# Four gelus that wait together for the last of four products

## The chip, the cores and the metric

The kernel runs on one core of a Trainium2 chip. A core has five engines with a queue of their own each: TensorE (PE; its weight loads are listed as PEld), VectorE (DVE), ScalarE (ACT), GpSimd (POOL) and SyncE (SP), which here only issues transfers. They meet through semaphores: an instruction can wait until a count is reached, and can raise a count when it is done. The metric is the time of one execution on the device in microseconds, lower is better.

## The reference, cut to what matters

The program is two layers of a graph network with attention and a mixture of experts, on 3125 nodes with 256 features. The change is in the last block of the second layer, a mixture of 8 experts of which each node uses two:

```
xn = layer_norm(x) * gamma + beta
logits = xn @ Wr + br                          # 8 logits a node
w = softmax of the two largest logits, 0 for the other experts
for e in range(8):
    h   = gelu(xn @ W1[e] + b1[e])             # 256 -> 512
    y_e = h @ W2[e] + b2[e]                    # 512 -> 256
    y  += y_e * w[..., e]
```

The kernel computes every expert for every node and weighs the results. All numbers are 32-bit floats.

## The kernel before, in words

Nodes lie in 25 tiles of 128 (the last has 53). The kernel makes two passes over the edges, one for each layer. A pass gathers, for each tile and each place in the nodes' edge lists, one row for every node from a table in memory (`gather`, L193, on GpSimd), and VectorE adds what came (L1356 folds the gathered rows, L1361 adds them to the tile's sum). The second pass runs from about 1590 us to the end. When a group of tiles has its sums, the rest of its work is put into a list of background jobs, and the pass does some of them after each handful of gathers, by a credit that the jobs' written costs use up.

There are 11 groups in the second pass. In order of work they have 4, 2, 4, 3, 3, 2, 2, 2, 1, 1 and 1 tiles. The jobs of a group (class `Group`) are: `sums_a` to `sums_c`, products of the graph part and a gelu (L2300 to L2309); `states_a` to `states_d`, the two normalizations, with square roots on ScalarE (L2327); `routes_a`, the transposes (L2370, L2371) and the eight logits (L2378); `routes_b`, the choice of two experts, with an exponential on ScalarE (L214); `shares`, a transpose of the weights (L2397, L2399) and the biases (L2425); then steps 0 to 9. The last four steps of a group are put between the first jobs of the next group.

Step i does three things in this order. `take` adds to x what the banks of earlier second products hold (L2450 for the biases, L2458 for an expert, VectorE). `hidden(i)` makes the first products of expert i for the whole group: 512 hidden features are four blocks of 128 (`FC` = 4), for each block two matmuls (one for each half of the 256 input features, L2408) fill one bank of PSUM, and ScalarE reads it through the gelu into `hT` (L2412). `outputs(i - 1)` makes the second products of the expert before (L2439): for each tile four matmuls, two tiles to a bank. A 32-bit matmul stands as two records in the trace, so `hidden` is 16 records and `outputs` 8 records for each tile.

The banks matter for the order. The pool `ps_mm` has four banks in turn; first products and the products of `sums_a` and `sums_b` share them. The second products use two other banks in turn (`bank`), and `hT` has three buffers. The order on VectorE and GpSimd is as the program is written (`manual_schedule`); the orders on TensorE and ScalarE are chosen by a planner from its own modelled times, with earlier written work first, so that an instruction which is ready sooner can be put ahead. ScalarE holds one table of functions at a time; gelu, exponential and square root need different ones, and a change of table is an instruction of its own (ACT_TABLE_LOAD).

Of the kernel before, what the change touches and what calls it, by code (L numbers as in the profile page):

```python
# [11 lines left out]
F32 = mybir.dt.float32  # L12
BF16 = mybir.dt.bfloat16
I32 = mybir.dt.int32
AF = mybir.ActivationFunctionType
# [5 lines left out]
P = 128  # L21
# [13 lines left out]
FC = F // P  # L35
# [65 lines left out]
def gps_kernel(ctx: ExitStack, tc: tile.TileContext, a, out):  # L101
    nc = tc.nc
    V, S, G, PE = nc.vector, nc.scalar, nc.gpsimd, nc.tensor
# [5 lines left out]
    ps_mm = ctx.enter_context(tc.tile_pool(name="ps_mm", bufs=4, space=PSUM))  # L109
# [1205 lines left out]

    def fast():
        fx = ExitStack()
        ek = fx.enter_context(tc.tile_pool(name="ek", bufs=1))  # L1320
# [175 lines left out]
        def hidden(ts):  # L1496
            n, at0 = len(ts) * P, ts[0] * P
            for i in range(2):
                hT = hTs[i] = f0h.tile([P, FC, 3 * P], F32, name=f"hT0_{i}", bufs=1)
                for f in range(FC):  # L1500
                    ph = ps_mm.tile([P, 512], F32, name="mm")
                    for c in range(2):
                        PE.matmul(  # L1503
                            ph[:, :n], w1[:, i, c, f * P : (f + 1) * P], xT[:, c, at0 : at0 + n],
                            start=(c == 0), stop=(c == 1),
                        )
                    S.activation(hT[:, f, :n], ph[:, :n], AF.Gelu, bias=b1[:, i, f : f + 1])

        def hidden_products(ts, i, ph=None):

            at0 = ts[0] * P
            ph = ps_mm.tile([P, 512], F32, name="mm") if ph is None else ph
            for f in range(FC):
                for c in range(2):
                    PE.matmul(
                        ph[:, f * P : (f + 1) * P], w1[:, i, c, f * P : (f + 1) * P], xT[:, c, at0 : at0 + P],
                        start=(c == 0), stop=(c == 1),
                    )
            return ph
# [45 lines left out]
        with ExitStack() as l0x:  # L1565
# [334 lines left out]
            def after0(g, tiles, accs):  # L1900
                last = g == len(GROUPS) - 1
                if last:
                    fin[0].accs = accs
                    return
                bg.extend(Fin0(tiles, accs).jobs())
                if g == SURE:
                    bg.extend(staged(guess(), (4.0, 3.0, 3.0, 2.0, 2.0, 2.0)))
                    for r in range(NX):
                        bg.extend(staged(relation(r), (1.5, 1.5)))
                for ts in GROUPS[: g + 1] if g == SURE else [tiles] if g > SURE else []:  # L1910
                    bg.append((5.0 * len(ts), lambda ts=ts: hidden(ts)))
                    if waiting:
                        bg.append(waiting.pop())
                    bg.append((4.0 * len(ts), lambda ts=ts: (outputs_a(ts), outputs_out(ts))))
                    waiting.append((1.0 * len(ts), lambda ts=ts: outputs_b(ts)))
                if g == len(GROUPS) - 2:
                    bg.append((4.0, lambda: None))
                    bg.append(waiting.pop())
                if g == len(GROUPS) - 2:
                    fin.append(Fin0(GROUPS[-1], None))  # L1920
                    bg.append((2.5, lambda: fin[0].products(0)))
# [21 lines left out]
            with tc.manual_schedule(engines={ET.DVE, ET.Pool, ET.PE, ET.Activation}):  # L1943
# [5 lines left out]
                phs = [hidden_products(ts, i) for i in range(2)]  # L1949
# [4 lines left out]
        with tc.If(again > 0):  # L1954
            w_full, rank = settled
            pick = f0k.tile([P, 2, NX], F32, name="pick")
            for i in range(2):
                V.tensor_scalar(pick[:, i, :], rank[:, 0, :], float(i), None, op0=ALU.is_equal)
            load_pair(pick)
            tmp = f0k.tile([P, NX], F32, name="tmp_c")  # L1960
            V.tensor_tensor(tmp, w_full[:, 0, :], pick[:, 0, :], op=ALU.mult)
            V.reduce_sum(w_first, tmp, axis=AX.X)
            for ts in GROUPS:
                k = len(ts)
                mv = small.tile([P, 4, 2], F32, name="mv1")
                rs = small.tile([P, 4], F32, name="rs1")
                for j, t in enumerate(ts):
                    V.tensor_tensor(x[:, t, :], x[:, t, :], bet, op=ALU.subtract)
                    stats(x[:, t, :], mv[:, j, :])
                rstd(mv[:, :k, :], rs[:, :k])  # L1970
                for j, t in enumerate(ts):
                    normalize(xt_tok[:, t, :], x[:, t, :], mv[:, j, :], rs[:, j : j + 1])
                    V.tensor_tensor(x[:, t, :], x[:, t, :], bet, op=ALU.add)
                    to_xT(t, xt_tok[:, t, :])
                if ts == GROUPS[-1]:
                    for i in range(2):
                        hidden_products(ts, i, phs[i])
                else:
                    hidden(ts)
                    outputs_a(ts)  # L1980
                    outputs_out(ts)
                    outputs_b(ts)
# [176 lines left out]
        with ExitStack() as l1x:  # L2159
# [18 lines left out]
            b1 = l1w.tile([P, NX, FC], F32, name="b1")  # L2178
# [107 lines left out]
            class Group:  # L2286
# [115 lines left out]
                def hidden(self, e):  # L2402
                    n, at0 = self.n, self.at0
                    hT = self.hT[e] = f1.tile([P, FC, 4 * P], F32, name="hT1")
                    for f in range(FC):
                        ph = ps_mm.tile([P, 512], F32, name="mm")
                        for c in range(2):
                            PE.matmul(  # L2408
                                ph[:, :n], w1s[e][:, c, f * P : (f + 1) * P], xT[:, c, at0 : at0 + n],
                                start=(c == 0), stop=(c == 1),  # L2410
                            )
                        S.activation(hT[:, f, :n], ph[:, :n], AF.Gelu, bias=b1[:, e, f : f + 1])  # L2412

                def bank(self):
                    turn[0] += 1
# [164 lines left out]
    with tc.If(unfit < 1):  # L2580
        fast()
# [78 lines left out]
```

## Time and profile before

| | |
|---|---|
| median of 4 runs | 2956.26 us (2943.61 to 2969.74) |
| profiled execution | 2937.95 us, span 2936.2 us |
| granted TensorE clock, mean of the span | 0.768 |
| gelus of the experts, L2412 | 352, 167.6 us busy, 496 ns each |
| table loads put down to L2412 | 27, 1283 ns each |
| first products, L2408 | 1408 records, 432.7 us busy |
| second products, L2439 | 1600 records, 405.4 us busy |
| weighted sums, L2458 | 200, 88.1 us busy, 478 ns each |

A row of the timeline gives start, duration, engine, line and operation, then the output and inputs by the program's names, the shapes, the number of instructions merged into the row, and in brackets how long the engine stood idle before it and what ended that. The ends of matmuls are modelled; their starts are recorded. A row of the waits gives the engine and line that waited, what it waited for, the total in microseconds, how often and the longest. "Issue" means that the profile shows nothing that was waited for, and "remote" that a semaphore ended the wait and no recorded instruction explains when.

### The profile page before, as it was taken

The page shows a single profiled execution, that of the slowest core. Times are in us where ns is not written, and L with a number is a line of the kernel's source. Part 1 is how long each engine was busy: PE and PEld are TensorE (multiplying, and loading weights), DVE is VectorE, ACT ScalarE, POOL GpSimd, SP SyncE. Part 2 cuts the span into 40 slices and gives each one's busy share as a digit, 9 for nine tenths or more (in the row PEclk, how much of TensorE's full clock was granted, in tenths as well). Part 3 has the DMA queues.
Part 4 walks back from the last instruction along what each step waited for, and adds up shares of the span by engine and source line. Part 5 has one row for each costly group of instructions (what it writes and reads, how often), then busy time and mean ns, then how long its engine had stood idle before and what let it go on. Part 6 is the DMA issues. An engine that isn't in the chain of part 4 may idle for free.

```text
span 2936.2 us, 20996 instructions
## 1 busy us (share of the span) xinstructions
PE 1880.8 (64%) x6033; PEld 1177.0 (40%) x6033; DVE 1256.6 (43%) x3537; ACT 558.3 (19%) x1275; POOL 1725.0 (59%) x1830
## 2 busy tenths in 40 slices
PE   4355667403473745275997259867887686767877
PEld 3222333202341423144443125544554464555666
DVE  7443545436333424344664333335343334344342
ACT  5122221001110101021321112112112121222233
POOL 5566665676757565753046745555666566665551
PEclk9666767655786766686998668878887888887878
DMA  6533333343323233332356532222332232232220
GB/s 189 126 92 90 93 90 102 94 107 108 95 77 102 69 99 81 100 81 57 144 201 233 162 104 76 84 79 84 89 93 85 72 86 83 83 90 75 79 81 16
DMA packets 125962, 290.09 MB, mean 99 GB/s; under 512 B 41386, under 2 KB 63982, under 8 KB 122632
## 3 DMA queue, kind: packets, MB, share of 16 engines
q0 software_dynamic: 83184, 230.02, 28.7%
q1 hardware_dynamic: 38122, 55.88, 5.8%
q10 hardware_dynamic: 4526, 2.71, 0.3%
q8 instruction: 51, 0.84, 0.1%
q14 instruction: 79, 0.65, 0.1%
HBM read 249.07 MB, written 39.41 MB: 98 GB/s over the span
## 4 chain that ended last, share of the span: by engine, by line
PE 22%; issue 9%; another core or an unknown queue 8%; POOL 5%; DVE 5%; ACT 2%; DMA 1%; SPq 0%; DVEq 0%; POOLq 0%; ACTq 0%
PE mm L2408 9%; PE py L2439 6%; POOL gt L193 5%; PE mm L188 3%; DVE gt L1356 1%; DMA gt<-htab_f,idx2g 1%; PE pctx L2247 1%; DVE bnst L162 1%; PE pt L2378 1%; DVE x L2458 1%; DVE acc L1361 0%; PE mm L2302 0%; PE py L2425 0%; DVE x L2343 0%
## 5 line engine op out<-in xcount | busy, mean ns | idle before, releaser
L193 POOL DMA_INDIRECT gt<-btab,idx x814 | 802.5, 986 | 444.7 <-issue 222.9
L193 POOL DMA_INDIRECT gt<-htab_f,idx2g x742 | 732.1, 987 | 477.0 <-DVE acc L1361 249.0
L2408 PE MATMUL mm<-xT,w 128*128 128x256 f32 (+4 forms) x1408 | 432.7, 458 | 108.0 <-issue 59.5
L2439 PE MATMUL py<-w,hT 128*128 128x256 f32 (+1 forms) x1600 | 405.4, 406 | 78.6 <-issue 41.7
L1356 DVE TENSOR_TENSOR gt<-gt 128x256 f32<-128x256 f32 (+1 forms) x767 | 410.1, 535 | 70.2 <-DMA gt<-htab_f,idx2g 23.3
L2439 PEld LDWEIGHTS py<-w,hT 128*128 128x128 f32 (+1 forms) x1600 | 317.6, 202 | 159.1 <-issue 79.7
L2408 PEld LDWEIGHTS mm<-xT,w 128*128 128x128 f32 x1408 | 267.4, 217 | 249.5 <-issue 159.2
L2458 DVE SCALAR_TENSOR_TENSOR x<-py,wf,x 128x256 f32<-128x256 f32 x200 | 88.1, 478 | 495.8 <-remote 284.1
L2412 ACT ACTIVATE hT<-mm,b 128x256 f32<-128x256 f32 (+4 forms) x352 | 167.6, 496 | 588.0 <-PE mm L2408 262.9
L188 PE MATMUL mm<-w_rel,xT 128*128 128x512 f32 x400 | 178.1, 603 | 8.0 <-ACT xT L183 7.4
L1361 DVE TENSOR_TENSOR acc<-acc,gt 128x256 f32<-128x256 f32 x371 | 158.3, 427 | 23.3 <-DVE gt L1356 6.6
L1532 PE MATMUL mm<-w,hT 128*128 128x256 f32 x400 | 126.4, 474 | 61.7 <-issue 53.6
L1503 PE MATMUL mm<-xT,w 128*128 128x384 f32 (+2 forms) x320 | 110.8, 513 | 80.6 <-issue 34.9
L1532 PEld LDWEIGHTS mm<-w,hT 128*128 128x128 f32 x400 | 90.7, 237 | 111.4 <-issue 85.2
L188 PE MATMUL mm<-w_qkv,xT 128*128 128x512 f32 (+1 forms) x200 | 101.0, 627 | 38.9 <-issue 25.5
L188 PE MATMUL pt<-w_own,xT 128*128 128x256 f32 x100 | 42.2, 547 | 125.7 <-DVE acc L1845 71.1
L1503 PEld LDWEIGHTS mm<-xT,w 128*128 128x128 f32 x320 | 69.7, 242 | 121.1 <-issue 56.5
L188 PEld LDWEIGHTS mm<-w_rel,xT 128*128 128x128 f32 x400 | 75.9, 193 | 102.4 <-issue 88.2
L1863 PE MATMUL pmean<-ones,xt 128*128 128x1 f32 (+1 forms) x100 | 21.5, 319 | 131.3 <-DVE xt L171 130.8
L193 POOL DMA_INDIRECT gt<-htab_f,soon x72 | 73.6, 1023 | 46.3 <-issue 20.2
L1620 DVE COPY slots<-gt 128x4 f32<-128x4 f32 (+1 forms) x214 | 36.8, 172 | 119.4 <-DMA gt<-btab,idx 112.7
L188 PEld LDWEIGHTS pt<-w_own,xT 128*128 128x128 f32 x100 | 24.6, 271 | 140.6 <-DVE acc L1845 73.1
(436 smaller groups left out, 2117.2 us busy)
## 6 DMA issues: line engine op xcount, KB each, us to landing
htab_f<-hs SPq DMA_DIRECT2D x25, 1024.0 KB
gt<-btab,idx POOLq DMA_INDIRECT x814
gt<-htab_f,idx2g POOLq DMA_INDIRECT x742
w<-in_f_W_dram SPq DMA_DIRECT2D x20, 512.0 KB
ntab<-x SPq DMA_DIRECT2D x5, 640.0 KB
btab<-bs SPq DMA_DIRECT2D x5, 640.0 KB
x<-in_x_dram SPq DMA_DIRECT2D x4, 640.0 KB
otab<-xn SPq DMA_DIRECT2D x16, 128.0 KB
```

The source lines that it names most:

```text
L162: V.bn_stats(out=st, in_=src)
L188: PE.matmul(ps, lhs[:, c, t * P : (t + 1) * P], w[:, c, :], start=start and c == 0, stop=stop and c == 1)
L193: G.indirect_dma_start(out=dst, out_offset=None, in_=table, in_offset=bass.IndirectOffsetOnAxis(ap=idx, axis=0))
L1356: V.tensor_tensor(gt[:, :h, :], gt[:, :h, :], gt[:, m - h : m, :], op=op)
L1361: V.tensor_tensor(acc, own(t) if i == 0 else acc, gt[:, 0, :], op=op)
L1503: PE.matmul(ph[:, :n], w1[:, i, c, f * P : (f + 1) * P], xT[:, c, at0 : at0 + n], start=(c == 0), stop=(c == 1),)
L1532: PE.matmul(py[:, i * D : (i + 1) * D], hTs[i][:, f, j * P : (j + 1) * P], w2[:, i, f, :], start=False, stop=(f == FC - 1), skip_group_che ...
L1620: V.tensor_copy(slots_of[t][:, U - 1 - k1 : U - 1 - k0], gw[:, : k1 - k0, D])
L2408: PE.matmul(ph[:, :n], w1s[e][:, c, f * P : (f + 1) * P], xT[:, c, at0 : at0 + n], start=(c == 0), stop=(c == 1),)
L2412: S.activation(hT[:, f, :n], ph[:, :n], AF.Gelu, bias=b1[:, e, f : f + 1])
L2439: PE.matmul(py[:r, j * D : (j + 1) * D], hT[:, f, at : at + r], w2s[e][:, f, :], start=(f == 0), stop=(f == FC - 1),)
L2458: V.scalar_tensor_tensor(d, y, wf[:r, t, e : e + 1], d, op0=ALU.mult, op1=ALU.add)
```

## The change

The four banks of an expert are taken first and all eight matmuls are written ahead of the four gelus. Each gelu gets, beside its own bank, a wait for the last matmul of the last block. Since ScalarE then waits for the same count before the first gelu, the other three need no wait of their own, and of the four products only the last has to signal. The number of matmuls, of gelus and their sizes is as before.

```
+    def behind(ins, pe):
+        tc.add_manual_dep(
+            ins.ins, pe.ins.name, mybir.DependencyInfo(mybir.DependencyClass.Sync, mybir.DependencyReason.DATA),
+            reason="one signal for a row of products",
+        )
...
                 def hidden(self, e):
                     n, at0 = self.n, self.at0
                     hT = self.hT[e] = f1.tile([P, FC, 4 * P], F32, name="hT1")
-                    for f in range(FC):
-                        ph = ps_mm.tile([P, 512], F32, name="mm")
+                    phs = [ps_mm.tile([P, 512], F32, name="mm") for f in range(FC)]
+                    for f, ph in enumerate(phs):
                         for c in range(2):
-                            PE.matmul(
+                            end = PE.matmul(
                                 ph[:, :n], w1s[e][:, c, f * P : (f + 1) * P], xT[:, c, at0 : at0 + n],
                                 start=(c == 0), stop=(c == 1),
                             )
-                        S.activation(hT[:, f, :n], ph[:, :n], AF.Gelu, bias=b1[:, e, f : f + 1])
+                    for f, ph in enumerate(phs):
+                        got = S.activation(hT[:, f, :n], ph[:, :n], AF.Gelu, bias=b1[:, e, f : f + 1])
+                        behind(got, end)
```

## The prediction

> **What bounds the kernel now.** I read the table of busy time, the busy time by stretch, the waits of the second pass (from 1750 us to the end), and then the timeline of two engines around single experts. The four columns before the clock are busy time and instructions of TensorE (PE), its weight loads (PEld), VectorE (DVE), ScalarE (ACT) and GpSimd (POOL).
>
> ```profile
> PE 1880.8 (64%) x6033; PEld 1177.0 (40%) x6033; DVE 1256.6 (43%) x3537; ACT 558.3 (19%) x1275; POOL 1725.0 (59%) x1830
> ...
> 1750.00:2936.00 1186.00, 917.09 (x3361) 642.47 (x3361) 465.38 (x1220) 266.89 (x503) 679.58 (x691) 0.83 0.28 78
> ```
>
> In the second pass TensorE is recorded busy for 917 of 1186 us, at a granted clock of 0.83; ScalarE, whose gelus are moved, for 267 us only. So a gelu that starts later costs nothing by itself; it costs where somebody waits for it. Who waits for whom (total us, times, longest):
>
> ```profile
> DVE x L2458 <- remote: 284.1, 22, 24.7
> ACT hT L2412 <- PE mm L2408: 262.9, 127, 14.2
> ACT hT L2412 <- remote: 239.1, 42, 25.5
> POOL gt L193 <- DVE acc L1361: 232.0, 51, 16.3
> ...
> PEld mm L2408 <- ACT hT L2412: 32.8, 14, 5.6
> ...
> PE mm L2408 <- ACT hT L2412: 24.4, 11, 4.9
> ```
>
> Everybody waits for TensorE: the gelus, the weighted sums of VectorE (L2458), and through VectorE's queue the gathers of GpSimd. In the other direction TensorE waits for a gelu in 25 places, 57 us together. Those 25 are what the change touches. "Remote" stands for a signal that no row explains. An expert of a four-tile group in calm, TensorE first, then ScalarE:
>
> ```profile
> 2064.01 7.03 PE L2408 MATMUL mm<-xT,w 128*128 128x512 f32 x16
> 2070.88 7.07 PE L2439 MATMUL py<-w,hT 128*128 128x256 f32 x32
> ```
>
> ```profile
> 2065.99 0.69 ACT L2412 ACTIVATE hT<-mm,b 128x512 f32<-128x512 f32 x1 [8.00 <-issue]
> 2067.64 0.69 ACT L2412 ACTIVATE hT<-mm,b 128x512 f32<-128x512 f32 x1 [0.97 <-PE mm L2408]
> ...
> 2071.08 0.69 ACT L2412 ACTIVATE hT<-mm,b 128x512 f32<-128x512 f32 x1 [1.03 <-issue]
> ```
>
> Sixteen records (two for each matmul) are four products, one every 1.72 us; each gelu follows its product at once. And a two-tile group where the signals are late, again TensorE first:
>
> ```profile
> 1947.42 2.72 PE L2408 MATMUL mm<-xT,w 128*128 128x181 f32 x16
> 1949.98 3.75 PE L2439 MATMUL py<-w,hT 128*128 128x256 f32 x16
> ...
> 1960.18 1.57 PE L2408 MATMUL mm<-xT,w 128*128 128x181 f32 x4 [3.35 <-issue]
> 1965.13 1.27 PE L2408 MATMUL mm<-xT,w 128*128 128x181 f32 x3 [3.39 <-ACT hT L2412]
> ```
>
> ```profile
> 1951.99 0.41 ACT L2412 ACTIVATE hT<-mm,b 128x181 f32<-128x181 f32 x1 [7.64 <-remote]
> ...
> 1959.71 0.41 ACT L2412 ACTIVATE hT<-mm,b 128x181 f32<-128x181 f32 x1 [3.81 <-remote]
> 1964.67 0.41 ACT L2412 ACTIVATE hT<-mm,b 128x181 f32<-128x181 f32 x1 [4.54 <-remote]
> ...
> 1976.77 1.32 ACT L2412 ACTIVATE hT<-mm,b 128x181 f32<-128x181 f32 x4 [11.69 <-remote]
> ```
>
> The four products were through by 1950.14, yet their gelus start 3.5, 4.2 and 5.0 us apart (the second, left out, at 1955.48), the last 14.5 us late, and the next expert's products follow them one by one. The signal that came next, behind the sixteen records of the second products, took another 12 us. The busy time by stretch gives 21 records of TensorE from 1958 to 1980, at a clock of 0.50, against 165 from 2044 to 2092 at 1.00.
>
> **The change part by part.** The pass has 11 groups (two of four tiles, two of three, four of two, three of one) with 8 experts each: 88 experts, 352 gelus.
>
> *Signals of TensorE.* 88 x 4 become 88; 264 go. In the calm expert the 16 records take 6.87 us from the first start to the first start after them (2064.01 to 2070.88), 0.43 us each, and four of them signal. No gap is there to be won: value 0. Upper bound of the gain: where signals are late, a gelu waits for "remote" 42 times; three of four of those signals go (31), at the 4.2 us between such gelus that is 132 us, if signals and not products were what is slow. I take 0, by the nearest row, the calm one: and in the late stage four records with their signal take 4.2 us, sixteen with one signal 12: the lateness goes by records rather than by signals.
>
> [...]
>
> *Gelus later, within a group.* In the four-tile group the first three gelus start up to three products (5.2 us) later. The last one matters: now it starts with its product's end, then it comes after three others. Four in a row take some 4 x 0.69 = 2.8 us against 0.69: 2.1 us later. Its reader, the second products of that expert, stands behind the 6.9 us of the previous expert's second products and the 6.9 us of the next first products. The next first product needs bank 0, free 0.9 us after the last product, behind those same 6.9 us. One tile: four gelus take 1.65 us at 2907.09, after, some 1.7; cover 1.73 us of second products, and the next first products for the reader. Cost 0 in the 77 experts after a group's first; at the very end, where the second products of expert 7 follow those of expert 6 directly, under 0.2 us. If the cover went, it would be 0.9 us an expert, 69 us.
>
> *A group's first expert.* Here no second products lie between hidden(0) and hidden(1). Before, product 0 of expert 1 finds its bank free; after, it waits for a gelu that starts behind product 3, and for the table of gelu, which ScalarE swaps. In the last group:
>
> ```profile
> 2892.80 1.28 ACT L214 ACT_TABLE_LOAD   x1
> 2894.09 0.21 ACT L214 ACTIVATE t_w<-t_w 128x8 f32<-128x8 f32 x1
> 2894.32 1.28 ACT L2412 ACT_TABLE_LOAD   x1
> ```
>
> The router's exponential (L214) falls between gelu 0 and gelu 1, so the table is loaded three times. After, the order on ScalarE is the planner's again. Exponential first (load at 2892.80, between gelu 0 at 2892.41 and gelu 1 at 2895.61): one load (1.28 us) and its gelu (0.37) less before the routing weights: gain up to 1.9 us. Gelus first: the exponential waits for a load and four gelus, 1.28 + 1.65 in place of 0.37, some 3.2 us with the queues. Bounds for 11 groups: -21 to +35 us. Where the planner now has the exponential ready after gelu 0, it has it ready before product 3; I take -0.5 us a group, -5 us.
>
> *The wait of the first gelu.* Behind it on ScalarE's queue stand square roots (L2327, 33), the gelus of the graph sums (L2309) and the copies of the routing. Those that the planner leaves behind it wait up to 5.2 us longer in calm, and VectorE waits for them: it waited 15.0 us for L2327 in all. Doubled, +15; moved ahead of the gelus, -15. I take 0.
>
> *Late stages.* A product of the next expert waited for one gelu each; now all four wait for the signal of product 3, and then run 0.4 to 0.7 us apart behind the gelus. In the rows above the last product could have started at 1965.13 before, and some 3 x 0.41 = 1.2 us later after. For the 25 places: +0 (something else is late) to +1.8 us each (three gaps of 0.6, the spacing of queued four-tile gelus at 1816.67 and 1817.26; 45 in all); I take 0.5, +12 us.
>
> Sum: 0 + 0 - 5 + 0 + 12 = +7 us on the profiled execution, whose own time is 2937.95 us (span 2936.2 and 1.75 around it): 2945. It stood 18.3 us under the median of the four runs, 2956.26; the forecast is that median and 7: **2963 us**.
>
> [...]
>
> **The rivals.** *Signals are the slow thing.* For it: late gelus come at even distances, one signal apart. Against: the calm row, and the 12 us of sixteen records with one signal. It would cut 60 to 132 us: 2824 to 2896; where only part of the waits is on the path, 2900 to 2926.
>
> *Slower: banks are held longer.* All four banks of the pool stay taken until product 3 is signalled. Where its signal is late, TensorE can't start the next expert's first product under the gelus, and it runs ahead by 12 records less in groups of one or two tiles. It decides from the point where product 3 is signalled later than the previous expert's second products end (3.6 us in a two-tile group, 1.7 in a one-tile one). Price: the full 45 us, or 35 us if the gelus also push the exponentials back; both, 80: 2991 to 3036. For it: 25 such waits already. Against: in late stages TensorE is held anyway.
>
> *It does nothing.* The queue is in order, so the wait for product 3 may only gather what was late together: 2950 to 2965, a part of the forecast's case.
>
> **How the numbers follow.** Forecast with the neutral rival (2935 to 2985): 0.52. Slower by banks or order: 0.30. Faster by signals or table loads: 0.18. One per cent, 29 us, is about what a measurement of this kernel tells from no change. The range goes down to 2915, part of the faster case, and up to 3010, the upper price of one mechanism.
>
> **What would show it.** Right: 88 waits of ACT L2412 for TensorE, gelus in blocks of four, fewer than the 27 table loads at L2412, TensorE's calm spacing unchanged at 0.43 us, "remote" waits of about the same total for VectorE (284 us). Bank rival: waits of L2408 for ACT hT well over 57 us. Signal rival: VectorE's remote wait far under 284 us and a higher clock than 0.83. The prediction fails if the planner reorders TensorE's queue, or if the late signals depend on what is queued.

## The result, and the profile after

The changed kernel takes 2979.98 us in the median (2941.04 to 2997.75), the kernel before, beside it, 2961.63 us (2935.56 to 2983.58). The ratio is 1.004, with a 95% interval of 1.0025 to 1.0055: some 12 us slower (7 to 16). The ratio and its interval go by fast runs alone, which leave out those more than 1.5% above the fastest of their kernel (13 of the 52 of the changed kernel, 3 of the 78 of before); the medians of all runs, above, differ by 18 us. The forecast had 7 us more than before.

The profiled execution of the changed kernel took 2968.34 us (span 2966.6). Of the 30.4 us by which its span is longer than that of before, 13.3 lie ahead of the change: the first product of the second pass starts at 1770.18 us, before at 1756.86, and the code up to there is the same. I take it for scatter between executions: in the kernels below, whose code is also the same up to there, this start lies anywhere from 1765 to 1798 us. From that product to the end it is 1196.5 us against 1179.4: 17 us more.

The table of busy time, and the second pass in the busy time by stretch (the columns are TensorE, its weight loads, VectorE, ScalarE, GpSimd, then TensorE's granted clock, the DMA share and GB/s):

```profile
PE 1879.4 (63%) x6033; PEld 1184.2 (40%) x6033; DVE 1256.7 (42%) x3537; ACT 530.7 (18%) x1269; POOL 1725.2 (58%) x1830
...
1750.00:2967.00 1217.00, 913.37 (x3372) 646.98 (x3371) 475.98 (x1252) 242.92 (x502) 682.62 (x696) 0.83 0.27 78
```

The work is the same, except that ScalarE has six instructions fewer (1269 for 1275). TensorE works as long and at the same clock, 0.83; the pass is longer because TensorE stands still longer. The waits of the pass (total us, times, longest), with L2415 for the first products, L2420 for the gelus, L2467 for VectorE's weighted sums:

```profile
DVE x L2467 <- remote: 289.5, 25, 25.6
ACT hT L2420 <- remote: 258.0, 15, 42.4
...
ACT hT L2420 <- PE mm L2415: 227.7, 50, 11.4
...
PEld mm L2415 <- ACT hT L2420: 50.7, 19, 11.7
...
PE mm L2415 <- ACT hT L2420: 42.2, 14, 10.1
```

ScalarE now waits seldom and long, as it should: 50 and 15 waits for TensorE's signals where there were 127 and 42. In the traces 96 of the 1408 records of first products raise a semaphore and 89 gelus carry a wait; before, 335 and 332. So some 240 signals went, and not quite the 264 that the prediction counted. The total of the unexplained ("remote") waits did not fall with the number of signals, 258.0 us for 239.1, nor did VectorE's (289.5 for 284.1). What grew is TensorE's own wait for a gelu: 42.2 us in 14 places, before 24.4 in 11. The two last rows must not be added, as the prediction did ("25 places, 57 us together"): the timeline shows that every one of the 14 stalls of the matmuls stands beside one of the weight loads, since both queues stop at the same gelu. The same holds for the 11 and 14 of before.

**Where the stalls lie.** The view of waits puts some of these stalls under "issue". So I went by the timeline: each idle time of TensorE ahead of a first product counts that is put down to a gelu, or that ends within 0.25 us of a gelu's end. That makes 50.9 us in 19 places before. Sorted by expert: at expert 1 of a group, the one that finds the gelus of the group's first expert in its way, there were 0.7 us in all 11 groups before, and 18.5 us after. At all other experts there were 50.2 us before and 51.0 after. The second group of three tiles shows how. The timeline of before, TensorE first, then ScalarE (start, length, instruction, count, idle time ahead of it):

```profile
2361.13 6.83 PE L2408 MATMUL mm<-xT,w 128*128 128x384 f32 x16
2367.79 0.49 PE L2397 MATMUL pt<-ident,wf 128*8 128x128 f32 x3
2368.12 1.46 PE L2408 MATMUL mm<-xT,w 128*128 128x384 f32 x4
```

```profile
2362.84 1.28 ACT L2412 ACT_TABLE_LOAD   x1 [3.46 <-PE mm L2408]
2364.13 0.58 ACT L2412 ACTIVATE hT<-mm,b 128x384 f32<-128x384 f32 x1
2364.73 1.28 ACT L214 ACT_TABLE_LOAD   x1
2366.02 0.22 ACT L214 ACTIVATE t_w<-t_w 128x24 f32<-128x24 f32 x1
2366.26 1.28 ACT L2412 ACT_TABLE_LOAD   x1
2367.56 0.58 ACT L2412 ACTIVATE hT<-mm,b 128x384 f32<-128x384 f32 x1
```

Three table loads, all while TensorE is still at the products of experts 0 and 1: gelu 0 has freed its bank by 2364.71, and nothing stops. The same group after the change:

```profile
2379.60 7.12 PE L2415 MATMUL mm<-xT,w 128*128 128x384 f32 x14
2386.56 0.49 PE L2404 MATMUL pt<-ident,wf 128*8 128x128 f32 x3
2388.73 0.91 PE L2415 MATMUL mm<-xT,w 128*128 128x384 f32 x2 [1.68 <-ACT hT L2420]
```

```profile
2377.14 1.28 ACT L214 ACT_TABLE_LOAD   x1
2382.16 0.22 ACT L214 ACTIVATE t_w<-t_w 128x24 f32<-128x24 f32 x1 [3.74 <-DVE t_w L213]
2386.80 1.28 ACT L2420 ACT_TABLE_LOAD   x1 [4.42 <-PE mm L2415]
2388.10 0.58 ACT L2420 ACTIVATE hT<-mm,b 128x384 f32<-128x384 f32 x1
```

The exponential (L214) now comes first and one table load less is needed. But the load that is left starts at 2386.80, once product 3 is signalled. All four banks are full; TensorE has three transposes (L2404) left to do, and stands still until 1.28 us of load and 0.58 us of gelu are over. In ten of the eleven groups this stall is 1.49 to 1.90 us; in the first it is 0.34. The groups of table loads on ScalarE show the saving that was forecast, 27 down to 21, and no gain shows for it:

```profile
L2420 ACT ACT_TABLE_LOAD x21 | 26.9, 1283 | 56.9 <-PE mm L2415 46.8 <-remote 9.9
```

These two profiles alone don't show that the stall at expert 1 is the loss. TensorE's idle time ahead of first products, whatever ended it, is 108.0 us before and 107.0 after: the part under "issue" that ends with no gelu fell from 33.0 to 6.5 us between the two executions. What the stall costs is shown by the times of the kernels below.

### The profile page after: what moved, and what is told of

It reads as the page before. It is cut to its first block, busy times and chain, and to the rows that moved or that the text cites. A ratio compares the mean times of both kernels' runs of the same rounds, so it can differ in the third digit from the quotient of the medians.

```text
span 2966.6 us, 20994 instructions
## 1 busy us (share of the span) xinstructions
PE 1879.4 (63%) x6033; PEld 1184.2 (40%) x6033; DVE 1256.7 (42%) x3537; ACT 530.7 (18%) x1269; POOL 1725.2 (58%) x1830
## 4 chain that ended last, share of the span: by engine, by line
PE 23%; another core or an unknown queue 9%; issue 9%; DVE 5%; POOL 3%; ACT 3%; DMA 1%; DVEq 0%; ACTq 0%; POOLq 0%
PE mm L2415 8%; PE py L2448 6%; PE mm L188 5%; POOL gt L193 3%; DVE gt L1363 1%; ACT hT L2420 1%; PE pt L2385 1%; DVE bnst L162 1%; DVE x L2467 1%; PE mm L2309 1%; DMA gt<-htab_f,idx2g 0%; ACT L2420 0%; PE py L2434 0%; PE mm L2307 0%
## 5 line engine op out<-in xcount | busy, mean ns | idle before, releaser
L2415 PE MATMUL mm<-xT,w 128*128 128x256 f32 (+4 forms) x1408 | 425.2, 458 | 107.0 <-ACT hT L2420 42.2
L2448 PE MATMUL py<-w,hT 128*128 128x256 f32 (+1 forms) x1600 | 395.9, 400 | 92.1 <-issue 42.2
L2415 PEld LDWEIGHTS mm<-xT,w 128*128 128x128 f32 x1408 | 271.8, 220 | 241.1 <-issue 118.3
L2467 DVE SCALAR_TENSOR_TENSOR x<-py,wf,x 128x256 f32<-128x256 f32 x200 | 88.1, 479 | 516.7 <-remote 289.5
L2420 ACT ACTIVATE hT<-mm,b 128x256 f32<-128x256 f32 (+4 forms) x352 | 147.6, 496 | 552.7 <-remote 258.0
L1510 PE MATMUL mm<-xT,w 128*128 128x384 f32 (+2 forms) x320 | 118.6, 538 | 113.0 <-issue 82.0
L1510 PEld LDWEIGHTS mm<-xT,w 128*128 128x128 f32 x320 | 72.1, 252 | 158.5 <-issue 110.1
L1870 PEld LDWEIGHTS pmean<-ones,xt 128*128 128x128 f32 (+1 forms) x100 | 23.0, 317 | 140.7 <-DVE xt L171 136.8
```

The source lines that it names most:

```text
L1510: PE.matmul(ph[:, :n], w1[:, i, c, f * P : (f + 1) * P], xT[:, c, at0 : at0 + n], start=(c == 0), stop=(c == 1),)
L1870: PE.matmul(pmean[0][:, c : c + 1], xt_tok[:r, t, c * P : (c + 1) * P], ones[:r, 0:1], start=(t in (1, SEEN + 1) and c == 0), stop=(t in ( ...
L2415: end = PE.matmul(ph[:, :n], w1s[e][:, c, f * P : (f + 1) * P], xT[:, c, at0 : at0 + n], start=(c == 0), stop=(c == 1),)
L2420: got = S.activation(hT[:, f, :n], ph[:, :n], AF.Gelu, bias=b1[:, e, f : f + 1])
L2448: PE.matmul(py[:r, j * D : (j + 1) * D], hT[:, f, at : at + r], w2s[e][:, f, :], start=(f == 0), stop=(f == FC - 1),)
L2467: V.scalar_tensor_tensor(d, y, wf[:r, t, e : e + 1], d, op0=ALU.mult, op1=ALU.add)
```

## The experiments

The theory that I began with: signals cost nothing, and the loss comes from banks that are held until product 3 is signalled, in late stages and in small groups. The rivals: signals matter; the order of the instructions matters. All ratios are to the kernel before on the same chip. The forecasts give TensorE's waits as the sum of the two rows of the view of waits (57 us before, 93 after), which counts the same stalls twice. What I give as measured goes by the timeline, as above: "stalls at expert 1" and "at other experts".

**Order without the common wait.** The products are still written ahead of the gelus; the added wait is gone.

```diff
                         got = S.activation(hT[:, f, :n], ph[:, :n], AF.Gelu, bias=b1[:, e, f : f + 1])
-                        behind(got, end)
```

> The four first products of an expert are written ahead of the four gelus, as in the changed kernel, but each gelu waits for its own product again, so TensorE gives four signals per expert. Theory of the held banks (mine): what costs is the common wait, so this kernel takes 1.000 of the time before (0.999 to 1.001), and TensorE waits for gelus for about the 57 us of before, not the 93 us of after. Rival, the planner: the cost comes from the order in which the instructions are written and planned; then it stays near the 1.004 of the changed kernel, with some 93 us of such waits. Rival, signals are worth something: it would be slower than the changed kernel, above 1.004, because it gives back the four signals and keeps the order.

Measured: 0.9979 (0.9944 to 1.0015), clear of the 1.0025 at which the interval of the changed kernel begins. The stalls at expert 1 are 8.5 us, at other experts 47.1, with 27 table loads at the gelus. So the order in which the lines are written costs nothing that shows; the common wait does.

**Four signals again, the common wait kept.** For each of the first three products of an expert an empty instruction on SyncE waits.

```diff
+                    ends = []
...
+                        ends.append(end)
+                    for one in ends[:-1]:
+                        behind(nc.sync.nop(), one)
```

> The changed kernel, with an empty instruction on SyncE that waits for products 0, 1 and 2 of each expert: TensorE signals all four again, while the gelus still wait for the last. It measures the price of 264 signals alone. Held banks (mine): signals cost nothing, so 1.004 of the time before, as the changed kernel (1.003 to 1.006), with about 93 us of TensorE waiting for gelus. [...] SyncE's queue takes 88 waits more, which may delay its loads; a longer wait for loads would show that.

Measured: 1.0042 (1.001 to 1.0074), the same as the changed kernel. Its waits:

```profile
ACT hT L2424 <- remote: 281.0, 16, 40.9
ACT hT L2424 <- PE mm L2416: 245.3, 51, 11.4
...
PE mm L2416 <- ACT hT L2424: 51.9, 14, 16.9
```

358 records of first products raise a semaphore here, against 96. With these signals back, the gelus' waits and TensorE's stalls at expert 1 (18.6 us) are those of the changed kernel. The value 0 stands within what these intervals can tell, and the upper bound of 132 us is out.

**Two signals, two waits of two gelus each.**

```diff
+                    ends = {}
...
-                            end = PE.matmul(
+                            ends[f] = PE.matmul(
...
-                        behind(got, end)
+                        behind(got, ends[f | 1])
```

> The changed kernel with two signals per expert: gelus 0 and 1 wait for product 1, gelus 2 and 3 for product 3. Held banks (mine): the delay of the first gelu is a third of that in the changed kernel and the last three of four free their bank nearly as before, so a third to a half of the loss, 1.001 to 1.003, with 65 to 80 us of TensorE waiting for gelus. Rival, the planner's order: no different from the changed kernel, 1.004. Rival, signals are worth something: 176 fewer signals at no delay give a gain, below 1.000.

Measured: 0.9979 (0.9943 to 1.0015). I had expected a third to a half of the loss; all of it is gone. The stalls at expert 1 are 2.4 us. As the edit has it, gelu 0 and its table load start at product 1, so that two products cover them.

**Where it costs.** Four kernels with the new form in a part of the experts only, and the old form (the old lines, gelu after product) in the rest: in groups of up to two tiles, of three and four, at expert 0 of each group, at experts 1 to 7. The edit is one condition.

```diff
                 def hidden(self, e):
...
+                    if not (self.k <= 2):  # or: self.k >= 3; e == 0; e > 0
+                        for f in range(FC):
+                            ph = ps_mm.tile([P, 512], F32, name="mm")
...
+                            S.activation(hT[:, f, :n], ph[:, :n], AF.Gelu, bias=b1[:, e, f : f + 1])
+                        return
```

> The common wait and the one signal only in the seven groups of one and two tiles (56 of 88 experts); the groups of three and four tiles are written as before. Held banks (mine): in the small groups an expert's first products are short and little work of TensorE covers the gelus, so most of the loss of the changed kernel is here: 1.002 to 1.005 of the time before, and TensorE's waits for gelus stay near 90 us. Rival, the large groups' longer products delay the gelus longer (5.2 us against 1.3 us), so the loss is there: then this one is at 0.999 to 1.001.

> The common wait and the one signal only in the four groups of three and four tiles (32 of 88 experts); the small groups as before. Held banks (mine): the second products cover the later gelus, so 1.000 (0.999 to 1.002), TensorE's waits for gelus near the 57 us of before. Rival, the loss follows the length of the products: 1.003 or more.

> The common wait and the one signal only for expert 0 of each group (11 of 88), where no second products lie between the first products of experts 0 and 1. My sum has a gain of 5 us here: six table loads fewer (1.28 us each, 27 becomes about 21 at the gelus), the exponential ahead of the gelus, so 0.997 to 1.000. Rival, the planner's order is what costs: all of the moved instructions of the changed kernel are in these places, so this one has its whole loss, 1.003 to 1.005.

> The common wait and the one signal only for experts 1 to 7 of each group (77 of 88); the first expert as before. Held banks (mine): the whole loss of the changed kernel without the small gain at the first experts, 1.004 to 1.006, TensorE's waits for gelus near 90 us, and 27 table loads at the gelus. Rival, the planner's order: 0.999 to 1.001.

Measured:

| new form in | ratio (95%) | stalls at expert 1 | at other experts | gelu table loads |
|---|---|---|---|---|
| no expert (before) | 1 | 0.7 us | 50.2 us | 27 |
| all (the change) | 1.004 (1.0025 to 1.0055) | 18.5 | 51.0 | 21 |
| small groups | 1.0007 (0.9979 to 1.0035) | 13.1 | 26.5 | 25 |
| large groups | 1.0015 (0.9986 to 1.0043) | 17.0 | 38.9 | 23 |
| expert 0 | 1.0027 (0.9997 to 1.0058) | 23.0 | 28.6 | 21 |
| experts 1 to 7 | 0.9973 (0.9943 to 1.0003) | 2.2 | 80.6 | 27 |

By size of group nothing is settled: both ratios lie between 1 and the changed kernel's, and their intervals touch either. (Of the 17.0 us of the large groups' row, 5.4 lie in these groups; more than half of the rest are two stalls of over 3 us in small groups where the gelus were late.) The two last rows are the reverse of what I had expected. With the new form at 11 experts the ratio is near that of all 88, though its interval still takes in 1; with the new form at the other 77 there is no loss. The intervals of these two touch at their ends. The time goes with the stalls at expert 1 (23.0 and 2.2 us), not with those at the other experts (28.6 and 80.6). The kernel with the new form at experts 1 to 7 is instructive, since in the very execution that shows the longest stalls of this table,

```profile
PEld mm L2425 <- ACT hT L2430: 77.7, 9, 21.9
PE mm L2425 <- ACT hT L2430: 73.1, 8, 21.5
```

the whole program took 2939.85 us, near the fastest. So there the end did not wait for the stalls in these places; the packed kernels below suggest why. My theory was wrong about the place, the late stages, and another took over: the loss is the common wait at expert 0, where a table load stands behind it with all banks full.

**More room in the banks.** A bank of the kernel's pool is 512 numbers of a partition (`ps_mm.tile([P, 512], F32)`); the blocks of a one-tile group are 128 wide, of a two-tile group up to 256. Here they share banks, so that an expert takes one or two of the four, and the common wait stays.

```diff
-                    phs = [ps_mm.tile([P, 512], F32, name="mm") for f in range(FC)]
+                    each = min(FC, 512 // (self.k * P))
+                    banks = [ps_mm.tile([P, 512], F32, name="mm") for f in range(0, FC, each)]
+                    phs = [banks[f // each][:, f % each * self.k * P :] for f in range(FC)]
```

> The changed kernel, with the first products of the groups of one tile all four in one bank and those of two tiles two in a bank; groups of three and four tiles keep one bank each. The one signal and the common wait stay. With eight rotating banks unchanged, the next expert's first products find a free one earlier. Held banks (mine): TensorE's waits for gelus fall well under the 93 us of the changed kernel, below 57 us of before as well, and the time is 1.000 or lower (0.995 to 1.001). Rival, the lateness of the signals itself: the gelus come late whatever the banks, the time stays at 1.003 to 1.005, and the idle time of TensorE moves from the first products to the second ones, which wait for the same gelus.

Measured: 0.9976 (0.9939 to 1.0013), clear of the changed kernel. (The pool has four banks, not the eight of the expectation.) No stall for a gelu is left at the other experts, and of those at expert 1, 5.4 us, all in the groups of three and four tiles, which weren't packed. In the last group the load of the table is as late as in the changed kernel, and TensorE goes on (TensorE first, then ScalarE):

```profile
2913.45 6.60 PE L2417 MATMUL mm<-xT,w 128*128 128x128 f32 x36
```

```profile
2916.87 1.28 ACT L2422 ACT_TABLE_LOAD   x1 [1.39 <-PE mm L2417]
2918.16 0.37 ACT L2422 ACTIVATE hT<-mm,b 128x128 f32<-128x128 f32 x1
```

Thirty-six records without a gap, over load and gelu. A part of the waiting moved to the second products, as the rival had it (24.7 us in 5 places, 11.1 in 1 in the changed kernel), without taking the gain back.

**The table loaded ahead.** A tiny gelu behind the exponential, and the gelus of expert 0 behind it; its result is unused.

```diff
-        S.activation(w, w, AF.Exp)
+        expo[:] = [S.activation(w, w, AF.Exp)]
...
+                    warm = fin.tile([P, 1], F32, name="warm")
+                    self.warm = S.activation(warm, b1[:, 0, 0:1], AF.Gelu)
+                    behind(self.warm, expo[0])
...
                         behind(got, end)
+                        if e == 0:
+                            behind(got, self.warm)
```

> The changed kernel, with one tiny gelu (128x1, its result unused) on ScalarE right behind the router's exponential of each group, and the gelus of expert 0 held behind it, so that the table of gelu is loaded (1.28 us) while the first products of expert 0 still run. In the earlier runs the stretch from expert 0 to expert 1 took 82 to 92 us in 11 groups where expert 0 kept its own waits, 106 us in the changed kernel. Theory now: at expert 0 the table load of 1.28 us stands between the one signal and the first gelu, and TensorE waits for it with all four banks full. Then this run gives back about 1.3 us of the 1.9 us a group: a sum near 92 us, and 0.999 to 1.001 of the time before. Rival, it is not the load but the four full banks alone: then the sum stays at 104 to 108 us and the time at 1.003 to 1.005. Second rival, the loss is not at expert 0 at all: the sum falls and the time stays at 1.004.

Measured: 1.000 (0.996 to 1.0039). The same group as above, TensorE, then ScalarE:

```profile
2378.66 6.55 PE L2420 MATMUL mm<-xT,w 128*128 128x384 f32 x14
2385.05 0.49 PE L2409 MATMUL pt<-ident,wf 128*8 128x128 f32 x3
2386.10 1.56 PE L2441 MATMUL py<-b2a,wT 8*128 8x256 f32 x6 [0.56 <-ACT wT L2411]
```

```profile
2381.48 1.28 ACT L2401 ACT_TABLE_LOAD   x1
2382.78 0.20 ACT L2401 ACTIVATE warm<-b 128x1 f32<-128x1 f32 x1
2385.58 0.47 ACT L2411 COPY wT<-pt 8x384 f32<-8x384 f32 x1 [2.60 <-PE pt L2409]
2385.96 1.96 ACT L2425 ACTIVATE hT<-mm,b 128x384 f32<-128x384 f32 x4
```

The load runs under the products. The stalls at expert 1 are 1.2 us in all, the 18.5 are gone, and so is the loss, though the interval alone does not exclude all of it (it ends at 1.0039). The sum from expert 0 to expert 1 that I had named as the mark did not fall: it is 116.5 us, and 106.2 in the changed kernel. It was a bad mark. As the rows show, the planner put the products of the biases (L2441) ahead of expert 1's first products. It did so in eight of the eleven groups; in the changed kernel two or six records of expert 1 come first. And in two groups a late signal (6.62 us) and a late exponential (10.67 us) fell into the stretch.

So this kernel changes two things, the load and the order on TensorE. TensorE's idle time from the last record of expert 0 to the last of expert 1 fell from 14.6 to 3.8 us in eight groups, and rose from 8.1 to 16.3 in the other three, the two with the late signal and the late exponential among them. That most of the stall is the load is read from the rows of the changed kernel (1.28 us of load, 0.58 of gelu); this kernel agrees with it, but doesn't part the load from the order.

**The cover taken away.** The gelus of experts 1 to 7 come behind the last second product of the expert before, too.

```diff
+                    self.held = (e, hT, phs, end)
+                    if e == 0:
+                        self.gelus_of(end)
...
-                        self.outputs(i - 1)
+                        last = self.outputs(i - 1)
+                        if i < NX:
+                            self.gelus_of(last)
```

> The changed kernel, with the gelus of experts 1 to 7 put behind the last second product of the expert before, too: the second products no longer cover them. It measures what the cover was worth in the step that was put at 0. By the prediction's price, 0.9 us for each of 77 experts, 69 us more than the changed kernel: 1.02 to 1.03 of the time before, with TensorE's waits for gelus far above 93 us. Rival, TensorE's idle time is made good behind it, because the sums of VectorE and the gathers set the pace: under 1.01.

Measured, in six runs only: 1.020 (1.0133 to 1.0266), 1.6% or 47 us over the changed kernel (28 to 67 by the ends of this interval). The waits:

```profile
ACT hT L2427 <- PE py L2455: 340.1, 43, 23.1
...
PEld mm L2415 <- ACT hT L2427: 156.1, 54, 18.9
PE mm L2415 <- ACT hT L2427: 134.3, 50, 18.5
```

At the other experts TensorE now stands 135.9 us for gelus, 85 more than in the changed kernel. So the second products do cover the later gelus; without them it is some 0.6 us of time an expert (47 us by 77), less than the 85 us of stalls.

**Both remedies, and packing alone.** Packed banks with the common wait at experts 1 to 7 only, and packed banks without any.

```diff
-                        behind(got, end)
+                        if e > 0:  # the other kernel: no line at all
+                            behind(got, end)
```

> The blocks packed into banks as in the packed run, the one signal for experts 1 to 7, and each gelu of expert 0 waiting for its own product as before the change. If the loss is expert 0's, this joins the two versions that ran at 0.9973 and 0.9976: 0.994 to 0.997 of the time before, the sum from expert 0 to expert 1 at 82 us or less. Rival, both runs were no more than scatter: 0.998 to 1.001.

> The blocks packed into banks, and each gelu waiting for its own product at every expert: no common wait, four signals. If what helps is that banks come free, it is as good as the run with one signal for experts 1 to 7 in packed banks (0.994 to 0.997). Rival, fewer signals at the later experts are a gain by themselves (0.2% to 0.3% by the run with only experts 1 to 7): then it stays at 0.998 to 1.000, slower than that one.

Measured: 0.9986 (0.9954 to 1.0019) and 0.998 (0.9948 to 1.0013). Neither reaches the 0.994 to 0.997, and they don't differ: one signal at the later experts is no gain that these runs can tell. There is no stall at expert 1 in either, so that remedy is used up. The second kernel is less than I had meant it to be: the timeline shows the gelus of a packed bank starting only after the last product in that bank (at expert 2 of the last group the four products end between 2918.67 and 2922.67, and the gelus start at 2922.76). So in one-tile groups it still has a common wait, and that costs nothing there, because the next expert has other banks.

It also bears on what a stall in a late stage is worth. It has 2.2 us of stalls for gelus in the whole pass, and yet TensorE stands still ahead of first products for 94.5 us under "issue" (33.0 before, 6.5 in the changed kernel). With everything else that ended such idle time it comes to 106.9 us, about the 108.0 and 107.0 of those two. One such stretch, TensorE, then ScalarE:

```profile
2654.82 3.62 PE L2417 MATMUL mm<-xT,w 128*128 128x256 f32 x16
2658.28 1.67 PE L2449 MATMUL py<-w,hT 128*128 128x256 f32 x7
...
2672.72 0.59 PE L2417 MATMUL mm<-xT,w 128*128 128x256 f32 x1 [2.23 <-issue]
2675.51 0.58 PE L2417 MATMUL mm<-xT,w 128*128 128x256 f32 x1 [2.20 <-issue]
2677.62 0.58 PE L2417 MATMUL mm<-xT,w 128*128 128x256 f32 x1 [1.52 <-issue]
```

```profile
2653.72 0.84 ACT L2422 ACTIVATE hT<-mm,b 128x256 f32<-128x256 f32 x2 [2.98 <-remote]
2683.29 2.29 ACT L2422 ACTIVATE hT<-mm,b 128x256 f32<-128x256 f32 x6 [28.73 <-remote]
```

All gelus that free the banks for the products of 2672.72 were done by 2654.56, so TensorE waits for no gelu; its records still start 2.1 to 2.8 us apart, and ScalarE hears of the products of 2654.82 at 2683.29. In this stretch TensorE is slow by itself, and a held bank would only change the name of its idle time. That this holds for all late stages is not shown.

No version is shown to be faster than the kernel before. Six are clear of the changed one: order alone, pairs, experts 1 to 7, and the three with packed banks. The profiled executions, one of each kernel, fit this on the whole when only the time from the first product to the end is taken, which leaves out the scatter ahead of it: 1179.4 us before; 1196.5 with the change, 1189.5 with four signals and the common wait, 1193.1 with the new form at expert 0, 1195.9 in large groups and 1180.0 in small ones; and 1162.7 to 1185.1 in the six and the kernel with the table loaded ahead.

## Why the prediction was right, and where it was not

The sum was +7 us, measured are +12 (7 to 16), and the case of 2935 to 2985 us was held the likeliest. That the sum came so near is luck: two of its terms were wrong in opposite directions, by some 23 and 12 us, and their errors half cancelled.

- **Signals of TensorE, 0.** Held, by the kernel with four signals and a common wait, to within these intervals. The calm expert of four tiles takes 7.03 us for its sixteen records, as before.
- **Gelus later within a group, 0.** Held. In calm the gelus come in a block of four (2.42 us at 2085.73) under the second products. Stalls at the experts other than expert 1 grew by 0.8 us in all. The price of the cover, put at 69 us, measured 47.
- **A group's first expert, -5.** This is the step that failed, in its last sentence: "I take -0.5 us a group". The order it forecast came about, exponential first and 27 loads down to 21. It counted the loads and did not ask which of them TensorE waits for. The ones that went had run under products; the one that stayed was moved behind the signal of product 3, where nothing covers it. Measured are 18 us of stalls in the profile, inside the bounds of -21 to +35 and of the other sign. The sentence ahead of it had all that was needed (product 0 of expert 1 "waits for a gelu that starts behind product 3, and for the table of gelu") and gave it no price: in the three-tile group 1.28 us of load and 0.58 of gelu, less the 0.33 that TensorE's transposes cover, are 1.5 us, and eleven of them 17 us.
- **The wait of the first gelu, 0.** VectorE's waits for the square roots, which the term weighed, add to 17.2 us in the pass before (the prediction's 15.0 is the largest row, not all of them) and to 10.4 after. ScalarE's waits for VectorE at the square roots (L2334) grew from 53.6 to 82.3 us, and VectorE's for the exponential (L214) shrank from 35.9 to 19.8. That none of these reaches the end is argued only; no kernel tried it alone.
- **Late stages, +12.** Mis-sized: the new form at experts 1 to 7 alone costs nothing (0.9973), with 80.6 us of stalls there. The 25 places were counted in two queues, and a late gelu in such a stage can find TensorE slow already, as in the stretch of the packed kernel without common waits. The prediction had that as its lower bound.

Of the rivals, "signals are the slow thing" is out. "Banks are held longer" had the right mechanism in the wrong place. Its sign showed (by the same count of two queues, 93 us of waits where 57 had been), but it put the point of decision at late signals, while it decides where no second products lie between two experts, and its price was some 17 us by the stalls, not 35 to 80. With the stalls added at expert 1, up to 1.90 us long, the pass keeps its clock of 0.83.

## What to carry to other kernels

Before gelus (or any readers of product banks) are made to wait together, look for the iteration that has no other work of TensorE behind it, here the first of a group, and lay ScalarE's queue out there: the signal, a table load if one is due, the first reader, and only then is a bank free. What a table load cost here went by where it stood, not by the count: six loads fewer (27 to 21, 1.28 us each) gained nothing, and the one behind the common signal, with the gelu after it, stopped TensorE for 1.49 to 1.90 us in ten of eleven groups. In this kernel a tiny activation, two waits in place of one, or blocks that share a bank took away the stall (of 18.5 us at expert 1, 1.2, 2.4 and 5.4 were left, the 5.4 in groups that were not packed). And two queues that stop at one signal are one stall: each of the 14 stalls of the matmuls stood beside one of the weight loads.

## What the runs showed that I had not expected

TensorE was slow here with nothing to wait for that the profile names. In the stretch above, of the packed kernel without common waits, it did thirteen records from 2660.76 to 2681.81 us, 1.6 us each, where the sixteen of 2654.82 took 3.62 together, and the signal of products that had ended by 2658.44 reached ScalarE at 2683.29, 25 us later. TensorE's granted clock was 0.63 from 2658 to 2683 us, and 1.00 in the 17 us ahead. Such stretches are in every kernel here. One of them lies in the same place in all fourteen, in the third group of the pass, between the first products of experts 3 and 5 (from 2106 us before, from 2121 in the first packed kernel; before, the granted clock was 0.69 from 2106 to 2126 us); others come and go. Their cause is not settled by these runs. The number of signals seems not to be it: sixteen "remote" waits of the gelus with four signals an expert and the common wait add to 281.0 us, the fifteen with one to 258.0.

A table load took 1.28 us and started 0.02 us after the end of the activation ahead of it, and the next activation started 0.01 us after it (2364.71 to 2364.73 and 2366.01 to 2366.02, in the first fence of ScalarE above). So the switch of tables took 1.31 us there, and the 1.28 us of the load is the price put on the stalls above.
